# Edge loops of a graph network that load and store two chunks at a time

## The chip, the cores and the metric

The kernel runs on one core of a Trainium2 chip. A core has five engines that each work through a program of their own: TensorE (PE, with its weight loads shown apart as PEld), VectorE (DVE), ScalarE (ACT), GpSimd (POOL) and SyncE (SP, which here only issues DMAs). They wait for each other by semaphores. The metric is the time of one execution in microseconds, lower is better: before the change the median of three runs is 10,185.69 us (10,173.44 to 10,188.64).

## What is computed

A graph has 10,000 nodes and 160,000 edges with 64 features each. The edges come sorted by the node that they point to (`dst`). Two networks run over it, one behind the other. What matters of the reference:

```python
def _genconv(x, src, dst, ea, W1, b1, lg, lb, W2, b2, t):
    m = jax.nn.relu(x[src] + ea) + EPS
    logits = m * t
    mx = jax.ops.segment_max(logits, dst, num_segments=N)
    e = jnp.exp(logits - mx[dst])
    denom = jax.ops.segment_sum(e, dst, num_segments=N)
    alpha = e / denom[dst]
    agg = jax.ops.segment_sum(m * alpha, dst, num_segments=N)
    h = agg + x
    h = h @ W1 + b1
    h = jax.nn.relu(_ln(h, lg, lb))
    return h @ W2 + b2
...
x = x @ encW + encb
ea = edge_attr @ eencW + eencb
x = _genconv(x, src, dst, ea, ...)               # layer 0
for i in range(1, 4):                            # layers 1 to 3
    h = jax.nn.relu(_ln(x, normG[i], normB[i]))
    x = x + _genconv(h, src, dst, ea, ...)
x = jax.nn.relu(_ln(x, normG[0], normB[0])) @ linW + linb
...
# then, with x as it was plus this result, layer-normed and rectified, as h:
score = Kh[src] * Qh[dst] * inv_sqrt_d * Eh      # 8 heads of 8 features
score = jnp.exp(jnp.clip(score.sum(-1, keepdims=True), -5.0, 5.0))
wV = jax.ops.segment_sum(Vh[src] * score, dst, num_segments=n)
```

The output is `x + wV`, 10,000 rows of 64 floats. So there are five passes over all edges: four convolutions with a softmax over the edges of each node, and one attention.

## The kernel before

**Layout.** The edges are cut into two halves. The first half is walked forwards and the second backwards, side by side: a column of a tile holds 64 features of an edge of the first half in partitions 0 to 63, and 64 of an edge of the second in partitions 64 to 127. 128 columns are a group, four groups are a **chunk** (512 columns, 1024 edges). There are 625 groups and so 158 chunks: 155 of four groups, then one of two, one of two and one of one (L51). The function `span` (L759) gives a chunk's first group, its number of groups and its columns.

**Segments.** Maxima and sums over the edges of a node are scans along the columns on DVE. A row of marks, broadcast over 64 partitions for each half, tells the scan where a node ends. After each chunk the scans' states are transposed and written to DRAM as rows (`st0`, or `st1` in attention). When the loop is over, the node stage gathers for each node the row at which its edges ended.

**The stages in order.** A preparation (some 100 us) that finds the ends, then the edge loop of layer 0, a node stage (`node_layer`, L941 on), and so on through layer 3, then the edge loop of attention (`attention_layer`) and a short end.

**A chunk of `softmax_layer`** (L802 on):

- `fetch` (L812): SP loads the marks (`load_marks`, L792: two DMAs, one for each half, six buffers) and either the encoded edges' columns (`load_ea`, L763: one DMA of 256 KB from `eaT`, four buffers) or, in layer 0, the rows of the raw edge attributes (`load_rows`, L769: two DMAs, three buffers `er`).
- in layer 0 alone `turn_rows` (L779): eight matmuls turn the rows into columns in the bank `ept` (L784, L785), ACT copies them to an `ea` buffer (L788), and SP stores that to `eaT` for the layers after it (L789).
- `front` (L821): POOL issues eight indirect DMAs (L756), each of which gathers 128 rows of the nodes' table into one of seven `xg` buffers (a buffer holds a chunk's eight). PE adds the edges times their weights (L829) and the transposed rows (L831) in a PSUM bank `z`. ACT rectifies and scales (L834, L835), DVE scans for the running maximum (L841) with the marks, and ACT makes exponentials (L846 to L849). `z_bank` (L815) takes five banks by turns in layers 1 to 3 (three called `z`, then `ept` and `hist`) and three in layer 0, where the other two have other work.
- `decay` (L856) and `back` (L865), the latter one chunk later: DVE makes the running sums (L871, L874) and transposes them (L900) to one of three buffers `so`, and SP writes these by four DMAs of 128 KB (L904).

**The order.** Within a loop the helper `InOrder` (L79) binds the instructions of each engine to the order in which the program names them, so what is written first is issued first, also on SP. The loop of `softmax_layer` names, for chunk k: the fetch of chunk k+3 (`lead = 3`), the front of k, in layer 0 the turning of k+2, then the back of k-1 with its stores. So on SP the loads for k+3 stand ahead of the stores of k-1. In layer 0 PE and ACT also count nodes and encode them beside the edges; in layer 1 SP writes zeros to `qs` in every fourth chunk (`clear_queries`).

**A chunk of `attention_layer`**: the fetch of chunk k+2 (L1138) is one DMA of the queries' rows (`q`, three buffers under the tag `er`), two of marks and one of `ea`. `ahead` (L1145) turns and spreads the queries of k+1, `fetch_kv` issues eight gathers into four-row halves of the `xg` buffers (`kv`), `scores` (L1180 to L1185) and `weights` (L1191, L1192) make the exponentials, and `back` (L1199 to L1216) makes the running sums and stores them by four DMAs of 64 KB.

**Buffers shared with the node stage.** In `node_layer` the tile `n_g` for the gathered states takes the buffers of `so` (L956).

Of the kernel before, what the change touches and what calls it, by code (L numbers as in the profile page):

```python
# [9 lines left out]
F32 = mybir.dt.float32  # L10
BF = mybir.dt.bfloat16
# [5 lines left out]
P = 128  # L17
# [3 lines left out]
G = 128  # L21
CG = 4
# [4 lines left out]
def kernel(ctx: ExitStack, tc: tile.TileContext, a, out):  # L27
# [24 lines left out]
    NC = len(chunks)  # L52
    W = 1280
# [705 lines left out]
    def span(k):  # L759
        g0, n = chunks[k]  # L760
        return g0, n, slice(g0 * G, (g0 + n) * G)

    def load_ea(k):  # L763
        g0, n, cols = span(k)
        ea = edge.tile([P, CE], F32, name="ea", bufs=4)
        nc.sync.dma_start(ea[:, :n * G], eaT[:, cols])
        return ea

    def load_rows(k, ea_rows):  # L769
        g0, n, cols = span(k)  # L770
        er = edge.tile([P, 2, CG, D], F32, name="er", bufs=3)
        e1 = NE - g0 * G
        nc.sync.dma_start(er[:, 0, :n, :],
                          ea_rows[g0 * G:(g0 + n) * G, :].rearrange("(g p) d -> p g d", p=G))
        nc.sync.dma_start(er[:, 1, :n, :],
                          ea_rows[e1 - n * G:e1, :].rearrange("(g p) d -> p g d", p=G))
        return er

    def turn_rows(k, er):  # L779

        g0, n, cols = span(k)
        pt = ps("ept", [P, CE])
        for g in range(n):
            nc.tensor.matmul(pt[:D, g * G:(g + 1) * G], er[:, 0, g, :], ident, start=True, stop=True)  # L784
            nc.tensor.matmul(pt[D:, g * G:(g + 1) * G], er[:, 1, n - 1 - g, :], anti,  # L785
                             start=True, stop=True)
        ea = edge.tile([P, CE], F32, name="ea", bufs=4)
        nc.scalar.activation(ea[:, :n * G], pt[:, :n * G], AF.Copy)  # L788
        nc.sync.dma_start(eaT[:, cols], ea[:, :n * G])  # L789
        return ea  # L790

    def load_marks(k, rows):  # L792

        g0, n, cols = span(k)
        t = edge.tile([P, CE], BF, name="marks", bufs=6)
        for s in range(2):
            nc.sync.dma_start(t[s * D:(s + 1) * D, :n * G], rows[s:s + 1, cols].to_broadcast([D, n * G]))
        return t
# [3 lines left out]
    def softmax_layer(l, ea_rows=None):  # L802
# [9 lines left out]
        def fetch(k):  # L812
            return load_marks(k, ends_d), load_ea(k) if ea_rows is None else load_rows(k, ea_rows)
# [7 lines left out]
        def front(k, marks, ea):  # L821
            g0, n, cols = span(k)
            m = n * G
            xg = edge.tile([P, CG, 2, D], F32, name="xg", bufs=7)
# [40 lines left out]
        def back(k, z, u, dec, e):  # L865
# [32 lines left out]
            so = edge.tile([P, CE // 32, 2, 32], F32, name="so", bufs=3)  # L898
            for i, t in ((0, se), (1, sm)):
                V.transpose(so[:, :m // 32, i, :], t[:, :m].rearrange("p (b e) -> p b e", e=32))  # L900
            rows_out = st0[2 * g0 * G:2 * (g0 + n) * G, :].rearrange(
                "(b e s) (h x) -> s h e b x", e=32, s=2, h=2)
            for q in range(4):
                nc.sync.dma_start(rows_out[q // 2, q % 2],  # L904
                                  so[q * 32:(q + 1) * 32, :m // 32].rearrange("p b i c -> p b (i c)"))

        order = InOrder()
        def columns_of(k):
            return got[k][1] if ea_rows is None else turn_rows(k, got[k][1])

        lead = 3
        got = [fetch(k) for k in range(lead)]
        eas = [columns_of(k) for k in range(2)]
        held, counts = None, []
        for k in range(NC):
            if k + lead < NC:
                got.append(fetch(k + lead))
            z, u, up, e = front(k, got[k][0], eas[k])
# [21 lines left out]
    def node_layer(l):  # L940
# [13 lines left out]
        @stage  # L954
        def fetch(my, g, i0, n, c):
            my["g"] = t = edge.tile([P, GRP, D2], F32, name="n_g", tag="so", bufs=3)  # L956
            for i in range(n):
                gather(t[:, i, :], st0, ends[:, i0 + i:i0 + i + 1])
            if n % 2:
                V.memset(t[:, n, :], 1.0)  # L960
# [173 lines left out]
    def attention_layer():  # L1134
# [3 lines left out]
        def fetch(k):  # L1138
            g0, n, cols = span(k)
            q = edge.tile([P, CG, 2, D], F32, name="q", tag="er", bufs=3)  # L1140
            nc.sync.dma_start(
                q[:, :n], qs[2 * g0 * G:2 * (g0 + n) * G, :].rearrange("(g p s) d -> p g s d", p=G, s=2))
            return load_marks(k, keeps_d), q, load_ea(k)

        def ahead(k, keep, q, ea):  # L1145

            g0, n, cols = span(k)
            m = n * G
            pq = ps("oe", [P, CE])
# [45 lines left out]
        def back(k, keep, pv, sc):  # L1195
            g0, n, cols = span(k)
            m = n * G
            wv = ps("lg", [P, CE])
# [12 lines left out]
            so = edge.tile([P, CE // 32, 32], F32, name="so1", tag="so", bufs=3)  # L1211
            V.transpose(so[:, :m // 32, :], s[:, :m].rearrange("p (b e) -> p b e", e=32))  # L1212
            rows_out = st1[2 * g0 * G:2 * (g0 + n) * G, :].rearrange(
                "(b e s) (h c) -> s h e b c", e=32, s=2, h=2)
            for q in range(4):
                nc.sync.dma_start(rows_out[q // 2, q % 2], so[q * 32:(q + 1) * 32, :m // 32])  # L1216

        order = InOrder()
        got = [fetch(k) for k in range(2)]
        made = ahead(0, *got[0])  # L1220
        held = None
        for k in range(NC):
            kvs = fetch_kv(k)
            if k + 2 < NC:
                got.append(fetch(k + 2))
# [3 lines left out]
            held = got[k][0], pv, weights(k, psc)  # L1229
            if k + 1 < NC:  # L1230
                made = ahead(k + 1, *got[k + 1])
# [74 lines left out]
```

## Time and profile before

The profiled execution took 10,256.79 us, of which its span, from the first instruction to the last, is 10,254.7 us. The mean granted clock of TensorE in it was 0.629 of full speed.

| | before |
|---|---|
| median of 3 runs | 10,185.69 us |
| profiled execution | 10,256.79 us |
| instructions | 67,417 |
| bytes moved by DMA | 1103.63 MB, mean 108 GB/s |
| packets of the software queue (POOL's gathers) | 215,200, 12.6% of 16 DMA engines' span |
| stores of states, layers 0 to 3 | 2480 DMAs of 128 KB |
| loads of marks, layers 0 to 3 | 1240 DMAs of 64 KB |
| loads of `ea` | 620 DMAs of 256 KB |
| stores of states, attention | 652 DMAs of 64 KB |
| loads of edges' rows (`er`), layer 0 | 310 DMAs of 128 KB |

The counts of DMAs are those that the page lists for chunks of full size; the last three small chunks stand apart in it.

How to read the views. A row of a group names its line, engine and operation, what it writes and reads, how often it ran, its busy time and the mean of one instruction in ns; behind the bar stands the time for which its engine idled just before it, and what ended most of that. "Remote" there means that the releasing event could not be put to an instruction of the trace; "issue" is time in which the engine waited for nothing that the profile shows. A row of a timeline gives the start in us, the time, the engine, the line, the operation, a count, and in brackets the idle time before it. "SPq" is the queue of DMAs that SP issues; the time there is the time for which their issues stretch. A row of windows gives a stretch of time, its length and the busy time of each engine in it, then the granted clock, the busy share of the DMA engines, and GB/s.

### The profile page before, as it was taken

To read this page: it belongs to the slowest core of one execution; us is meant where nothing else is said; L and a number is where in the kernel's file an instruction comes from. 1 tells how busy PE (TensorE), PEld (TensorE's weight loads), DVE (VectorE), ACT (ScalarE), POOL (GpSimd) and SP (SyncE) were. 2 spreads that over 40 slices of the span, in tenths; PEclk is the share of its full clock that TensorE was granted. 3 is DMA by queue.
4 is the path that set the end of the run, shared out by engine and by line. 5 is a ranking of instruction groups with operands and counts; after the bars stand their busy time and mean duration, and the time that the engine had idled before them with its cause. 6 is when DMAs were issued, how large, how long until landed. Compare 5 with 4: busy or idle time off the path is not lost. (4 is left out here: it accounts for less than half of the span.)

```text
span 10254.7 us, 67417 instructions
## 1 busy us (share of the span) xinstructions
PE 4014.2 (39%) x15762; PEld 2685.3 (26%) x15762; DVE 5449.4 (53%) x7473; ACT 2805.0 (27%) x4803; POOL 6358.1 (62%) x6760
## 2 busy tenths in 40 slices
PE   3554445443333333433333343333333444444452
PEld 2333333222222221222222221222222233333331
DVE  3777677535555554355555543555555445545453
ACT  2333333333333333333333342333333310000000
POOL 4566666556666665566666646666666456666665
PEclk6666666665555556665666575555555667777776
DMA  3555555524555554244444433444444235555553
GB/s 89 113 125 123 123 124 123 123 59 119 125 125 129 128 124 109 62 102 105 104 104 103 105 78 71 105 105 104 103 104 106 62 92 122 125 123 126 122 128 82
DMA packets 2462634, 1103.63 MB, mean 108 GB/s; under 512 B 2039472, under 2 KB 2254438, under 8 KB 2462239
## 3 DMA queue, kind: packets, MB, share of 16 engines
q1 hardware_dynamic: 2247039, 827.14, 33.8%
q0 software_dynamic: 215200, 272.11, 12.6%
q8 instruction: 140, 2.29, 0.1%
q14 instruction: 255, 2.09, 0.1%
HBM read 626.51 MB, written 471.91 MB: 107 GB/s over the span
## 5 line engine op out<-in xcount | busy, mean ns | idle before, releaser
L756 POOL DMA_INDIRECT xg<-table,idxA x2500 | 2358.6, 943 | 1916.9 <-remote 829.7
L756 POOL DMA_INDIRECT xg<-table,idxB x2500 | 2358.8, 944 | 763.1 <-issue 761.2
L841 DVE TENSOR_TENSOR_SCAN u<-lg,u,marks 128x512 f32<-128x512 f32 (+1 forms) x628 | 798.5, 1272 | 2721.5 <-ACT lg L835 1612.7
L829 PE MATMUL z<-ea,eencW 128*128 128x512 f32 (+1 forms) x892 | 864.3, 1071 | 2137.1 <-DMA ea<-eaT 898.3
L831 PEld LDWEIGHTS z<-ident,xg 128*128 128x128 f32 x3512 | 800.4, 311 | 591.8 <-issue 566.5
L756 POOL DMA_INDIRECT kv<-kv_table,idxA x625 | 589.5, 943 | 439.7 <-remote 220.2
L831 PE MATMUL z<-ident,xg 128*128 128x128 f32 x3512 | 794.5, 395 | 162.0 <-DMA xg<-table,idxB 85.9
L829 PEld LDWEIGHTS z<-ea,eencW 128*128 128x128 f32 x892 | 222.2, 306 | 2231.8 <-issue 1981.7
L871 DVE TENSOR_TENSOR_SCAN se<-dec,se,e 128x512 f32<-128x512 f32 (+1 forms) x628 | 792.2, 1261 | 0.0
L874 DVE TENSOR_TENSOR_SCAN sm<-dec,sm,me 128x512 f32<-128x512 f32 (+1 forms) x628 | 782.3, 1246 | 0.0
L846 ACT ACTIVATE up<-lg 128x512 f32<-128x512 f32 (+1 forms) x632 | 374.3, 592 | 1352.9 <-issue 693.6
L756 POOL DMA_INDIRECT kv<-kv_table,idxB x625 | 589.7, 944 | 191.1 <-issue 190.2
L834 ACT ACTIVATE lg<-z 128x512 f32<-128x512 f32 (+1 forms) x446 | 249.4, 559 | 1555.8 <-remote 1032.3
L1185 PE MATMUL dec<-eq,head_sum 128*128 128x512 f32 (+2 forms) x316 | 237.1, 841 | 931.2 <-DVE eq L1183 887.1
L1192 ACT ACTIVATE sc<-sc 128x512 f32<-128x512 f32 (+1 forms) x158 | 98.7, 625 | 1744.7 <-DVE sc L1191 685.0
L784 PE MATMUL ept<-ident,er 128*64 128x128 f32 x1250 | 269.3, 380 | 752.4 <-ACT ea L788 517.7
L856 ACT ACTIVATE dec<-up 128x512 f32<-128x512 f32 (+1 forms) x632 | 377.1, 597 | 658.8 <-issue 561.0
L756 POOL DMA_INDIRECT n_g<-st,ends x316 | 300.8, 952 | 403.2 <-issue 142.2
L835 ACT ACTIVATE lg<-lg,teps,tcol 128x512 f32<-128x512 f32 (+1 forms) x632 | 471.4, 746 | 21.1
L829 PE MATMUL hist<-ea,eencW 128*128 128x512 f32 x186 | 189.5, 1123 | 709.5 <-DMA ea<-eaT 286.6
L829 PE MATMUL ept<-ea,eencW 128*128 128x512 f32 x186 | 185.5, 1100 | 710.3 <-DMA ea<-eaT 286.4
L1156 DVE TENSOR_TENSOR_SCAN qh<-marks,qh,oe 128x512 f32<-128x512 bf16 (+1 forms) x157 | 198.6, 1265 | 488.6 <-remote 389.8
(285 smaller groups left out, 8704.9 us busy)
## 6 DMA issues: line engine op xcount, KB each, us to landing
st<-so SPq DMA_DIRECT2D x2480, 128.0 KB
ea<-eaT SPq DMA_DIRECT2D x620, 256.0 KB
marks<-ends_d SPq DMA_DIRECT2D x1240, 64.0 KB
st<-so SPq DMA_DIRECT2D x652, 64.0 KB
xg<-table,idxA POOLq DMA_INDIRECT x2500
xg<-table,idxB POOLq DMA_INDIRECT x2500
qs<-zeros SPq DMA_DIRECT2D x40, 1000.0 KB
er<-in_edge_attr_dram SPq DMA_DIRECT2D x310, 128.0 KB
```

Of the source, the lines that this page charges most:

```text
L756: nc.gpsimd.indirect_dma_start(out=t, out_offset=None, in_=table, in_offset=bass.IndirectOffsetOnAxis(ap=idx, axis=0))
L784: nc.tensor.matmul(pt[:D, g * G:(g + 1) * G], er[:, 0, g, :], ident, start=True, stop=True)
L829: nc.tensor.matmul(z[:, :m], eencW, ea[:, :m], start=True, stop=False)
L831: nc.tensor.matmul(z[:, g * G:(g + 1) * G], xg[:, g, :, :].rearrange("p s d -> p (s d)"), ident, start=False, stop=(g == n - 1))
L834: S.activation(lg[:, :m], z[:, :m], AF.Relu)
L835: S.activation(lg[:, :m], lg[:, :m], AF.Identity, bias=teps[:, l:l + 1], scale=tcol[:, l:l + 1])
L841: V.tensor_tensor_scan(u[:, 1:m + 1], lg[:, :m], marks[:, :m], last, op0=OP.max, op1=OP.add)
L846: S.activation(up[:, :m], lg[:, :m], AF.Relu)
L856: S.activation(dec[:, :m], up[:, :m], AF.Exp, scale=-1.0)
L871: V.tensor_tensor_scan(se[:, :m], dec[:, :m], e[:, :m], prev.get("e", zero1), op0=OP.mult, op1=OP.add)
L874: V.tensor_tensor_scan(sm[:, :m], dec[:, :m], me[:, :m], prev.get("m", zero1), op0=OP.mult, op1=OP.add)
L1185: nc.tensor.matmul(psc[:, :m], head_sum, eq[:, :m], start=True, stop=True)
```

## The change

The chunks are put together in **units**: 78 pairs, and the last two chunks each alone, 80 in all. Loads and stores go by units, the computation still by chunks. `reach` gives a unit's first group, its groups and its columns; `within` gives the columns that a chunk has in a tile of its unit; `is_first` and `is_last` tell where in its unit a chunk stands.

- The tiles `ea`, `er`, `marks`, `q` and `so` are twice as long. Their buffers: `ea` 3 (before 4), `er` and `q` 2 (before 3), `marks` 3 (before 6), `so` 2 (before 3).
- In the loops, two units are fetched ahead of the first chunk; the fetch of unit u+2 is named at the last chunk of unit u, ahead of that chunk's front.
- `turn_rows` writes one half of a pair's `ea` at each chunk, and stores the pair's columns at its last chunk.
- The states of a pair are stored at its last chunk, by four DMAs of twice the size.
- `n_g` takes the buffers of `ea` in place of those of `so`.

The PE, ACT, DVE and POOL instructions of a chunk are the same as before, on slices of the longer tiles.

```diff
+    units = [[k, k + 1] for k in range(0, NC - 2, 2)] + [[NC - 2], [NC - 1]]
+    unit_of = {k: u for u, ks in enumerate(units) for k in ks}
...
-    def load_ea(k):
-        g0, n, cols = span(k)
-        ea = edge.tile([P, CE], F32, name="ea", bufs=4)
+    def reach(u):
+
+        g0 = chunks[units[u][0]][0]
+        n = sum(chunks[k][1] for k in units[u])
+        return g0, n, slice(g0 * G, (g0 + n) * G)
+
+    def within(k):
+
+        c = (chunks[k][0] - chunks[units[unit_of[k]][0]][0]) * G
+        return slice(c, c + chunks[k][1] * G)
+
+    def is_first(k):
+        return units[unit_of[k]][0] == k
+
+    def is_last(k):
+        return units[unit_of[k]][-1] == k
+
+    def load_ea(u):
+        g0, n, cols = reach(u)
+        ea = edge.tile([P, 2 * CE], F32, name="ea", bufs=3)
         nc.sync.dma_start(ea[:, :n * G], eaT[:, cols])
         return ea
 
-    def load_rows(k, ea_rows):
-        g0, n, cols = span(k)
-        er = edge.tile([P, 2, CG, D], F32, name="er", bufs=3)
+    def load_rows(u, ea_rows):
+        g0, n, cols = reach(u)
+        er = edge.tile([P, 2, 2 * CG, D], F32, name="er", bufs=2)
...
-    def turn_rows(k, er):
+    def turn_rows(k, er, ea):
 
         g0, n, cols = span(k)
+        in_unit = within(k)
+        first, total, unit_cols = reach(unit_of[k])
+        at = g0 - first
         pt = ps("ept", [P, CE])
         for g in range(n):
-            nc.tensor.matmul(pt[:D, g * G:(g + 1) * G], er[:, 0, g, :], ident, start=True, stop=True)
-            nc.tensor.matmul(pt[D:, g * G:(g + 1) * G], er[:, 1, n - 1 - g, :], anti,
+            nc.tensor.matmul(pt[:D, g * G:(g + 1) * G], er[:, 0, at + g, :], ident, start=True, stop=True)
+            nc.tensor.matmul(pt[D:, g * G:(g + 1) * G], er[:, 1, total - 1 - at - g, :], anti,
                              start=True, stop=True)
-        ea = edge.tile([P, CE], F32, name="ea", bufs=4)
-        nc.scalar.activation(ea[:, :n * G], pt[:, :n * G], AF.Copy)
-        nc.sync.dma_start(eaT[:, cols], ea[:, :n * G])
+        if ea is None:
+            ea = edge.tile([P, 2 * CE], F32, name="ea", bufs=3)
+        nc.scalar.activation(ea[:, in_unit], pt[:, :n * G], AF.Copy)
+        if is_last(k):
+            nc.sync.dma_start(eaT[:, unit_cols], ea[:, :total * G])
         return ea
 
-    def load_marks(k, rows):
-
-        g0, n, cols = span(k)
-        t = edge.tile([P, CE], BF, name="marks", bufs=6)
+    def load_marks(u, rows):
+
+        g0, n, cols = reach(u)
+        t = edge.tile([P, 2 * CE], BF, name="marks", bufs=3)
...
         def front(k, marks, ea):
             g0, n, cols = span(k)
             m = n * G
+            ea, marks = ea[:, within(k)], marks[:, within(k)]
...
-            so = edge.tile([P, CE // 32, 2, 32], F32, name="so", bufs=3)
+            if is_first(k):
+                prev["so"] = edge.tile([P, 2 * CE // 32, 2, 32], F32, name="so", bufs=2)
+            so, to = prev["so"], within(k)
             for i, t in ((0, se), (1, sm)):
-                V.transpose(so[:, :m // 32, i, :], t[:, :m].rearrange("p (b e) -> p b e", e=32))
-            rows_out = st0[2 * g0 * G:2 * (g0 + n) * G, :].rearrange(
+                V.transpose(so[:, to.start // 32:to.stop // 32, i, :],
+                            t[:, :m].rearrange("p (b e) -> p b e", e=32))
+            if not is_last(k):
+                return
+            first, total, _ = reach(unit_of[k])
+            rows_out = st0[2 * first * G:2 * (first + total) * G, :].rearrange(
                 "(b e s) (h x) -> s h e b x", e=32, s=2, h=2)
...
-        lead = 3
-        got = [fetch(k) for k in range(lead)]
-        eas = [columns_of(k) for k in range(2)]
+        got, eas = [fetch(u) for u in range(2)], []
+        for k in range(2):
+            eas.append(columns_of(k))
         held, counts = None, []
         for k in range(NC):
-            if k + lead < NC:
-                got.append(fetch(k + lead))
-            z, u, up, e = front(k, got[k][0], eas[k])
+            if is_last(k) and unit_of[k] + 2 < len(units):
+                got.append(fetch(unit_of[k] + 2))
+            z, u, up, e = front(k, got[unit_of[k]][0], eas[k])
...
-            my["g"] = t = edge.tile([P, GRP, D2], F32, name="n_g", tag="so", bufs=3)
+            my["g"] = t = edge.tile([P, GRP, D2], F32, name="n_g", tag="ea", bufs=3)
...
-            q = edge.tile([P, CG, 2, D], F32, name="q", tag="er", bufs=3)
+            q = edge.tile([P, 2 * CG, 2, D], F32, name="q", tag="er", bufs=2)
...
-            so = edge.tile([P, CE // 32, 32], F32, name="so1", tag="so", bufs=3)
...
+            if is_first(k):
+                prev["so"] = edge.tile([P, 2 * CE // 32, 32], F32, name="so1", tag="so", bufs=2)
...
         for k in range(NC):
             kvs = fetch_kv(k)
-            if k + 2 < NC:
-                got.append(fetch(k + 2))
+            if is_last(k) and unit_of[k] + 2 < len(units):
+                got.append(fetch(unit_of[k] + 2))
```

## The prediction

> **What bounds the kernel now.** I read the page first, then stretches by window, then the timelines of SP and POOL, then the waits. The page alone:
>
> ```profile
> span 10254.7 us, 67417 instructions
> PE 4014.2 (39%) x15762; PEld 2685.3 (26%) x15762; DVE 5449.4 (53%) x7473; ACT 2805.0 (27%) x4803; POOL 6358.1 (62%) x6760
> q1 hardware_dynamic: 2247039, 827.14, 33.8%
> L756 POOL DMA_INDIRECT xg<-table,idxA x2500 | 2358.6, 943 | 1916.9 <-remote 829.7
> L829 PE MATMUL z<-ea,eencW 128*128 128x512 f32 (+1 forms) x892 | 864.3, 1071 | 2137.1 <-DMA ea<-eaT 898.3
> ```
>
> POOL is the busiest engine, and nearly all it does is to issue row gathers at 943 ns. PE's largest idle time ends when a load of `ea` lands, and SP issues those. One window for each edge loop (layers 0 to 3, then attention) shows how near POOL is to being the limit:
>
> ```profile
> core 0: us, PE busy (x) PEld busy (x) DVE busy (x) ACT busy (x) POOL busy (x), PEclk, DMA share, GB/s
> 99.50:1956.20 1856.70, 885.59 (x5240) 633.47 (x5240) 1244.53 (x1819) 620.12 (x1062) 1178.44 (x1249) 0.64 0.54 118
> 2172.00:3953.40 1781.40, 564.79 (x1518) 365.15 (x1518) 921.23 (x1196) 539.71 (x902) 1178.32 (x1249) 0.56 0.50 121
> 4171.00:5946.50 1775.50, 566.99 (x1518) 367.63 (x1518) 921.35 (x1196) 539.54 (x902) 1178.49 (x1250) 0.60 0.44 100
> 6168.30:7944.50 1776.20, 568.30 (x1520) 367.93 (x1521) 922.19 (x1196) 539.55 (x902) 1179.27 (x1250) 0.56 0.44 100
> 8300.50:10112.00 1811.50, 878.62 (x4310) 650.56 (x4310) 904.24 (x1069) 96.34 (x153) 1180.17 (x1251) 0.73 0.52 124
> ```
>
> The five loops fill 9001 of 10,255 us. Each has 1250 gathers. Back to back they start 1.247 us apart (943 ns and 0.30 us between two), so 1250 take 1559 us: that is a loop's floor, 9.98 us for a chunk of eight. Length less floor is what can be won: 297 (of which about 74 lie before the first chunks flow), 222, 216, 217 and 252 us, 1204 in all. No other engine is near: DVE has 921 of 1776 us. What are POOL's pauses? Layer 2 in time, POOL and then SP:
>
> ```profile
> 4728.33 0.94 POOL L756 DMA_INDIRECT xg<-table,idxA  x1 [0.30 <-issue]
> 4729.58 0.94 POOL L756 DMA_INDIRECT xg<-table,idxB  x1 [0.30 <-issue]
> 4739.15 0.94 POOL L756 DMA_INDIRECT xg<-table,idxA  x1 [8.62 <-remote]
> ...
> 4719.71 5.65 SPq L904 DMA_DIRECT2D st<-so  x4
> 4725.38 1.46 SPq L797 DMA_DIRECT2D marks<-ends_d  x2
> 4728.92 0.71 SPq L766 DMA_DIRECT2D ea<-eaT  x1
> 4732.43 4.25 SPq L904 DMA_DIRECT2D st<-so  x4
> 4737.43 0.71 SPq L797 DMA_DIRECT2D marks<-ends_d  x2
> 4738.84 0.01 SPq L766 DMA_DIRECT2D ea<-eaT  x1
> 4746.51 2.25 SPq L904 DMA_DIRECT2D st<-so  x4
> 4748.81 1.29 SPq L797 DMA_DIRECT2D marks<-ends_d  x2
> 4750.20 0.52 SPq L766 DMA_DIRECT2D ea<-eaT  x1
> ```
>
> POOL runs six chunks and stops 8.6 us, because all seven `xg` buffers wait for PE. SP needs 12.7 us from one chunk's stores to the next (4719.7 to 4732.4) while POOL runs, and 7 us for the same seven DMAs (4746.5 to 4753.4) just after POOL has paused. So in layers 1 to 3 SP, at 12.7 us a chunk, is slower than POOL at 9.98, and PE gets `ea` at SP's pace. In layer 0 and attention SP has gaps and is not late: there SP's waits are for ACT's `ea` (570 us) and DVE's `so` (502 us).
>
> **The change, part by part.**
>
> *SP's DMAs, halved in number.* A chunk of layers 1 to 3 now costs SP 4 stores, 2 marks, 1 `ea`; layer 0 adds 2 `er` and 1 `eaT` store, attention adds 1 `q`: 7, 9 and 8 DMAs. With 80 units for 158 chunks they become 560 instead of 1106 in a loop of layers 1 to 3, 720 instead of 1422, 640 instead of 1264: 2964 fewer. An issue does not cost by its packets: the medians are 692 ns for a store (512 packets), 698 ns for marks (64), 586 ns for `ea` (128). So SP's slow pace falls from 12.7 us a chunk to about 6.4, below POOL's 9.98, and `ea` stops being late. What is late next is POOL itself and what makes it pause.
>
> Here a rule speaks against the change. The Trainium skill, "DMA: Bandwidth & Descriptors", section "Issuing engines are not separate DMA queues", holds that the sequencer's time to start a DMA is usually small beside the DMA. By that rule the 2964 issues hide and the sum is 0. The SP rows above say 12.7 us a chunk where POOL needs 9.98, so in layers 1 to 3 I follow the row; in layer 0 and attention, where SP idles, the rule stands for the issue time itself.
>
> *POOL's pauses.* Does removing SP's lateness remove the pauses? Not by itself. In the last fence PE had issued its matmuls on `ept` at 4704.4 (PE timeline), yet ACT's relu on that bank started at 4738.9, after 15.6 us of idling for "remote", 7 us after POOL stopped: results of PE become visible late while POOL runs without a break. Two bounds. If the pauses go with SP's DMA count (1.5 us in layer 0 for 9 DMAs, 1.37 for 7 in layers 1 to 3, 1.55 for 8 in attention: 0.17 to 0.20 us each), half of 1150 us goes: -575. If they are POOL's own, 0. The nearest rows are stretches with other DMA rates; the share of time POOL pauses beyond its 1.247 us steps, from POOL counts in windows and SP's timeline:
>
> - start of layer 2, 4172 to 4329.6 us: 112 gathers, 42 SP DMAs, 0.27 a us: 0.113
> - rest of layer 2: 1135 gathers, 990 DMAs, 0.61 a us: 0.122
> - attention from 8353 us: 1214 gathers, 0.69 a us: 0.139
> - layer 0 from 173 us: 1193 gathers, 0.75 a us: 0.165
>
> After the change all loops issue 0.31 to 0.38 DMAs a us, between the first two rows. I take 0.113 for layers 1 to 3 and the middle, 0.1175, for the others: 3 x 1778 x 0.0095 = 51; layer 0 1783 x 0.0475 = 85; attention 1759 x 0.0215 = 38. Sum **174 us**, far nearer the lower bound than -575, since the start of layer 2 pauses nearly as much with few DMAs.
>
> *Data.* Same bytes; rows of `ea` double to 4 KB and marks to 2 KB, the store rows stay 256 bytes. q1 has 24.7 ns a packet (33.8% of 16 engines' 10,255 us over 2.247 M). 90,000 packets fewer free 0.9% of the engines, which are 44 to 54% busy: 0 on the path. A doubled store of 1024 packets holds the engines 1.6 us instead of 0.8.
>
> *Stores moved to the second chunk of a pair.* Nobody reads `st` before the loop ends. The last two units are single chunks, so the tail is as before: 0.
>
> *Lead.* Before, chunk k+3 was fetched in iteration k, behind the stores of k-2. Now unit u+2 is fetched at the pair's second chunk, behind the stores of u-1: its first chunk is as far ahead as before, the second one chunk further. But four doubled stores stand ahead in the queue: 4 x 0.8 = 3.2 us later, in layer 0 also two `er` of 0.8 more: 4.8 us (estimates from q1). In layers 1 to 3 five z banks give PE's next `ea` five chunks' time: 0. In layer 0 (three banks, `er` two pairs deep) PE waited for `er` 39 times, 106.8 us; I count 0 there in the forecast because the second chunk of each pair no longer waits (gain at most 53 us against at most 39 x 4.8 = 187 lost); this cover is the rival below.
>
> *Buffers.* `so` two pairs (four chunks, before three), marks three pairs (six, as before), `q` and `er` two pairs (four, before three), `ea` three pairs: none tighter, and the reader of the oldest is done before SP reaches the fetch. `n_g` moves from `so` to `ea`: its first gathers wait for all stores either way; the next loop's first two `ea` loads wait for the last `n_g` to be divided, which ends some 20 us before the loop. 0. DVE, ACT and PE run the same instructions.
>
> The sum is against the profiled execution (10,256.8 us with its ends); the median of the runs is 0.7% lower, so 174 becomes 173 and 10,185.7 becomes **10,013**; I say 10,010.
>
> **Rivals.**
>
> *SP was the limit all along.* For it: in loop 2 PE waits for `ea` or marks before almost every chunk, SP is the only engine with a pace over 11.4 us. Against it: layer 0 and attention pause more, with SP idle. Then the pauses halve: 10,186 - 571 = 9615.
>
> *Slower: the first chunk of each pair in layer 0 comes late.* The queue is in order, so `er` of the pair stands behind four doubled stores and feeds PE's turn, which stands ahead of the next z. At the 39 waits of today, 4.8 us each: +187, so 10,375; if all 79 pairs wait 7.5 us, +486. It decides once the delay exceeds what seven gathered `xg` chunks cover for POOL. Against it: layer 0 paces at 11.6 us and three banks leave over 20 us from one fetch to its use.
>
> *Nothing.* The pauses are POOL's and the DMA counts do not matter: 10,186.
>
> **How the numbers follow.** Forecast 0.36, SP the limit 0.23, slower 0.30, nothing 0.11. No change means within 0.2%, about what three runs that agree within 15 us can tell. Of "nothing", 0.06 stays within, 0.03 falls faster and 0.02 slower: faster 0.62, same 0.06, slower 0.32. The range reaches past 9615 on one side and to 10,380 on the other, leaving out the far ends of the two outer cases, some 0.2 together.
>
> **What would show it.** SP's rows per pair: four stores, two marks, one `ea` within 13 us, in 22 us. PE's wait for `ea` in layers 1 to 3 mostly gone. If POOL's 8.6 us pauses stay, still 12% of a loop, with PE's relu waits on "remote", the pauses are POOL's own; if they halve, SP's count was the cause. Wrong would be a layer 0 window above 1857 us with PE waiting for `er` more than 250 us, or loops 1 to 3 under 1690 us.

## The result: no gain

The changed kernel takes 10,193.33 us in the median of 12 runs (10,180.23 to 10,211.44), beside 10,185.64 us of 12 runs before. The ratio is 1.0009 with a 95% interval of 1.0000 to 1.0018: about 8 us longer if anything, where 173 us less were forecast. In the sittings of this study the kernel before took from 10,180 to 10,254 us, so a ratio is always to the runs of its own sitting. The profile of before that stands above took 10,256.79 us, longer than all 12 of these runs; a second one (run before_again below) took 10,177.53 us and is the one to set beside the profile after, 10,180.23 us.

From the page of the changed kernel, the rows that answer to those shown of before:

```profile
span 10178.3 us, 61984 instructions
PE 3875.6 (38%) x15762; PEld 2575.4 (25%) x15762; DVE 5448.0 (54%) x7473; ACT 2803.8 (28%) x4803; POOL 6360.2 (62%) x6760
q1 hardware_dynamic: 2099775, 826.95, 34.3%
L759 POOL DMA_INDIRECT xg<-table,idxA x2500 | 2358.5, 943 | 1853.3 <-issue 671.8
```

The change does what it says: 5433 instructions fewer, 3803 of them SP's (2964 DMAs, as counted, the rest semaphore instructions), and 147,264 packets fewer on SP's queue at the same bytes. POOL's gathers still take 943 ns each, and POOL idles nearly as long ahead of them. One window for each edge loop of the changed kernel, from first to last gather (length, then busy time of each engine, clock, DMA share, GB/s):

```profile
99.70:1930.20 1830.50, 866.81 (x5240) 616.79 (x5240) 1242.67 (x1820) 618.91 (x1063) 1179.54 (x1250) 0.65 0.57 120
2164.50:3926.60 1762.10, 526.11 (x1518) 334.40 (x1518) 924.48 (x1199) 540.78 (x905) 1179.23 (x1250) 0.58 0.50 122
4148.90:5914.60 1765.70, 518.94 (x1518) 331.50 (x1518) 919.14 (x1192) 537.83 (x899) 1179.25 (x1250) 0.59 0.43 100
6135.00:7901.80 1766.80, 523.19 (x1538) 334.13 (x1538) 922.28 (x1196) 539.66 (x902) 1179.27 (x1250) 0.59 0.44 100
8252.00:10039.90 1787.90, 889.84 (x4311) 656.56 (x4312) 908.25 (x1073) 96.34 (x153) 1180.40 (x1251) 0.73 0.52 126
```

From first to last gather, in us, beside the second profile of before:

| loop | before_again | after | from its last gather to the next stage's first, before_again | after |
|---|---|---|---|---|
| layer 0 | 1827.7 | 1829.5 | 56.5 | 67.0 |
| layer 1 | 1768.3 | 1761.1 | 54.3 | 55.4 |
| layer 2 | 1764.0 | 1764.6 | 54.2 | 58.9 |
| layer 3 | 1763.1 | 1765.8 | 54.3 | 54.8 |
| attention | 1790.4 | 1786.9 | 29.7 | 28.1 |

The loops did not move (8913.5 against 8907.9 us in sum), though SP has half as many DMAs in each. What moved most is the stretch behind layer 0, by 10.5 us. So there are two questions: why do POOL's pauses not care for SP, and what became late behind layer 0?

Here is how a pause of the changed kernel looks, in layer 2: rows from the timelines of SP, of PE and of POOL.

```profile
4461.26 3.47 SPq L936 DMA_DIRECT2D st<-so  x4
4464.77 2.63 SPq L822 DMA_DIRECT2D marks<-ends_d  x2
4467.52 0.84 SPq L786 DMA_DIRECT2D ea<-eaT  x1
4504.00 3.41 SPq L936 DMA_DIRECT2D st<-so  x4
```

```profile
4480.16 2.08 PE L855 MATMUL z<-ea,eencW 128*128 128x512 f32 x2 [4.69 <-issue]
4482.03 0.42 PE L857 MATMUL z<-ident,xg 128*128 128x128 f32 x1
4483.79 0.37 PE L857 MATMUL z<-ident,xg 128*128 128x128 f32 x1 [1.34 <-issue]
4485.89 0.37 PE L857 MATMUL z<-ident,xg 128*128 128x128 f32 x1 [1.73 <-issue]
...
4495.68 0.37 PE L857 MATMUL z<-ident,xg 128*128 128x128 f32 x1 [0.82 <-issue]
```

```profile
4487.98 0.94 POOL L759 DMA_INDIRECT xg<-table,idxB  x1 [0.30 <-issue]
4496.64 0.94 POOL L759 DMA_INDIRECT xg<-table,idxA  x1 [7.71 <-PE z L857]
```

SP issues nothing between 4468 and 4504, so its issues hold nobody up there. `ea` was there: PE's first matmul of the chunk runs at 4480. Yet its eight matmuls on `xg`, which take 1.05 us elsewhere in the same loop, take 14 us, with idle time that ends in "issue", that is, nothing that the profile shows.

And what does POOL wait for? It stops ahead of the loop's chunk 31 (the first is 0), which takes the `xg` buffer that chunk 24 had, seven before it. PE's matmuls on chunk 24, and ACT's first instruction on it:

```profile
4460.74 1.91 PE L857 MATMUL hist<-ident,xg 128*128 128x128 f32 x8
4496.40 0.58 ACT L860 ACTIVATE lg<-hist 128x512 f32<-128x512 f32 x1 [13.29 <-PE z L857]
```

PE had read the buffer by 4462.7, before POOL stopped at all. ACT idles for 13 us and begins on that chunk at 4496.4 and POOL goes on at 4496.6, both 34 us after PE's end. So POOL does not wait for PE to read; what PE has done is seen late. It is so at all 27 pauses over 1 us that stand ahead of a chunk of this layer: POOL goes on 31 to 74 us after PE's last read of the buffer. ACT starts 26 us after PE's last matmul on its chunk in the median of this layer, and 74 at most. The rows themselves are not late: by the packets of the software queue a gather is complete 2.2 us after its start in the median of this layer, and 4.2 at most.

### The profile page after: what moved, and what is told of

Its sections match the earlier page's. It is cut to its first block, busy times and chain, and to the rows that moved or that the text cites. A ratio compares the mean times of both kernels' runs of the same rounds, so it can differ in the third digit from the quotient of the medians.

```text
span 10178.3 us, 61984 instructions
## 1 busy us (share of the span) xinstructions
PE 3875.6 (38%) x15762; PEld 2575.4 (25%) x15762; DVE 5448.0 (54%) x7473; ACT 2803.8 (28%) x4803; POOL 6360.2 (62%) x6760
## 4 chain that ended last, share of the span: by engine, by line
issue 27%; DVE 21%; another core or an unknown queue 14%; POOL 11%; PE 10%; SPq 9%; ACT 4%; DMA 3%; DVEq 0%; ACTq 0%; POOLq 0%
POOL xg L759 10%; SPq L936 4%; DVE u L867 3%; SPq L822 3%; DVE sm L900 3%; DVE so L928 2%; DVE lg L869 2%; DVE se L897 2%; PE dec L1222 2%; PE z L1217 2%; DVE me L895 1%; PE oe L1188 1%; DVE qh L1193 1%; PE z L857 1%
## 5 line engine op out<-in xcount | busy, mean ns | idle before, releaser
L855 PE MATMUL z<-ea,eencW 128*128 128x512 f32 (+1 forms) x892 | 811.9, 1010 | 1866.4 <-issue 954.9
L857 PEld LDWEIGHTS z<-ident,xg 128*128 128x128 f32 x3512 | 753.4, 286 | 869.2 <-issue 827.1
L869 DVE TENSOR_TENSOR lg<-lg,u 128x512 f32<-128x512 f32 (+1 forms) x632 | 438.2, 693 | 21.9
L471 DVE TENSOR_TENSOR onehot_lo<-oe,lo_b 128x640 bf16<-128x640 f32 (+1 forms) x278 | 205.7, 740 | 429.2 <-remote 406.6
```

What stands on the lines that cost most here:

```text
L855: nc.tensor.matmul(z[:, :m], eencW, ea[:, :m], start=True, stop=False)
L857: nc.tensor.matmul(z[:, g * G:(g + 1) * G], xg[:, g, :, :].rearrange("p s d -> p (s d)"), ident, start=False, stop=(g == n - 1))
L869: V.tensor_sub(lg[:, :m], lg[:, :m], u[:, 0:m])
```

## The experiments

Two theories follow. **SP**: the packets of SP's DMAs (the stores are still 2048 packets a chunk) hold PE up. **POOL**: its own stream of gathers does, whatever SP issues. Most kernels below use layers 1 to 3 as three arms, since these loops are alike (1761, 1765 and 1766 us). Lengths are from a loop's first gather to its last.

**before_again**: the kernel before, unedited.

> The kernel before, profiled once more, to see how far two profiles of the same kernel differ. Every theory: the five edge loops (first to last gather) again near 1857, 1780, 1774, 1774 and 1810 us; if the whole is near the median of 10,186 us instead of 10,257, each loop may be some 14 us shorter (70 us over five loops).

10,177.53 us; the table above has its loops. They are 10 to 29 us shorter than in the first profile, more than the expected 14 in layer 0 and attention, less in layers 1 to 3.

**sp_off**: layer 1 stores nothing, layer 2 loads marks and `ea` once, layer 3 does neither.

```diff
+        kept = []
+
         def fetch(u):
+            if l in (2, 3):
+                if not kept:
+                    kept.append((load_marks(u, ends_d), load_ea(u)))
+                return kept[0]
...
-            if not is_last(k):
+            if not is_last(k) or l in (1, 3):
                 return
```

> The changed kernel with three arms, one in each of the layers 1 to 3 (it leaves out work there, so what these layers compute is not the reference's): layer 1 stores no states; layer 2 loads marks and ea once and uses them for all units; layer 3 does neither, so that SP has next to nothing to do. Changed kernel: 1761, 1765 and 1766 us from first to last gather. Theory SP (packets of SP's DMAs hold up PE and so POOL; the change halved DMAs but left 2048 store packets a chunk): layer 3 falls to the floor of POOL, 1560 to 1610 us, layer 1 most of the way, layer 2 stays. Theory POOL (POOL's own stream of gathers slows what PE's results take to be seen, whatever SP does): all three stay within 30 us of 1765.

Windows of its layers 1 to 3:

```profile
2164.80:3924.20 1759.40, 621.90 (x1539) 387.80 (x1540) 924.67 (x1199) 541.89 (x905) 1179.61 (x1250) 0.54 0.30 79
4097.60:5849.70 1752.10, 622.44 (x1548) 388.75 (x1548) 927.36 (x1203) 543.57 (x908) 1179.53 (x1250) 0.54 0.32 68
6081.90:7838.40 1756.50, 625.17 (x1538) 389.40 (x1538) 922.94 (x1196) 540.77 (x902) 1179.44 (x1250) 0.54 0.12 24
```

In layer 3 the DMA engines are busy for 12% of the time in place of 44%, with almost nothing but gathers, and the loop is 10 us shorter. POOL's pauses are still there (195 us). The theory SP falls for layers 1 to 3. For layer 0 and attention no run takes SP's DMAs away; there the change itself, which halves them, is the test, and it moved their loops by less than 4 us.

**pool_arms**: layer 1 gathers for every second chunk only, layer 2 gets a small memset on POOL ahead of each gather, in layer 3 PE turns one of four groups.

```diff
+            if l == 1 and not is_first(k):
+                xg = prev["xg"]
+            else:
...
+                        if l == 2:
+                            nc.gpsimd.memset(filler, 0.0)
...
-            for g in range(n):
+            for g in range(n if l != 3 else 1):
...
```

> The changed kernel with three arms (it leaves out work in layers 1 and 3): layer 1 gathers only for the first chunk of each pair, the second uses the same rows; layer 2 gathers all, with a small memset on POOL ahead of each of the 1250 gathers; layer 3 gathers all, but PE turns only one of four groups. Changed kernel: 1761, 1765 and 1766 us. Theory POOL (a backlog that fills while POOL issues gathers without a break, drained at about one gather in 1.41 us): layer 1 falls under 1250 us; in layer 2 the memsets take the place of the pauses, the loop stays within 60 us of 1765 and pauses over 1 us fall under 60 us in sum; layer 3 falls under 1650 only if PE's number of instructions is what fills the backlog, else it stays within 30 us. Theory SP: layer 2 becomes longer by all its memsets (at an estimated 0.2 us each +250, so 2015) and layer 3 stays.

1063.3, 1771.0 and 1723.2 us. Layer 1 speaks for POOL. Layer 2 says less than was meant: the memset of 127 ns fits into the 0.30 us between two gathers, POOL's step became 1.255 us, and pauses over 1 us still make 112. Layer 3 fell into neither number: 43 us shorter, no pause over 1 us, and POOL's median step was 1.397 us. Relieved of PE, POOL did not run at 1.247: it became slow itself.

**knee**: one, two and three memsets of 128x160 ahead of each gather.

```diff
+                    for _ in range(l):
+                        nc.gpsimd.memset(filler, 0.0)
                     gather(xg[:, g, s, :], tables[l], index(g0 + g, s))
```

> The changed kernel with POOL slowed by memsets of 128x160 ahead of each gather: one in layer 1, two in layer 2, three in layer 3 (their time is not known; by the 128x16 memset at 127 ns some 0.28 us each is an estimate, which makes POOL's step between gathers about 1.40, 1.75 and 2.1 us where it was 1.247). Theory POOL (a gather costs about 1.405 us in the long run, 1761 to 1766 us for 1250, and a burst at 1.247 is only borrowed): a loop takes the larger of 1760 us and 1250 of its own steps: layer 1 about 1760 without pauses over 1 us (under 60 us in sum), layers 2 and 3 their steps, 2190 and 2620, without pauses, and PE's and SP's slow steps gone there. Rival (the pauses come from PE's own lateness, a fixed share of about 12% of the time): each loop takes its own steps plus 12%: 1970, 2450, 2940.

Windows of its layers 1 to 3 (POOL's count has the memsets in it):

```profile
2164.80:3936.60 1771.80, 510.12 (x1519) 322.18 (x1520) 927.34 (x1203) 547.18 (x908) 1498.02 (x2500) 0.59 0.47 122
4148.30:6265.00 2116.70, 741.55 (x1560) 379.08 (x1560) 957.32 (x1243) 567.92 (x937) 1787.78 (x3749) 0.50 0.35 86
6448.80:8932.40 2483.60, 743.98 (x1562) 379.04 (x1562) 957.84 (x1244) 568.80 (x938) 2077.20 (x4997) 0.50 0.30 73
```

The steps came out at 1.362, 1.644 and 1.934 us. Layer 1 has 319 us more work on POOL than the changed kernel and is 10 us longer: its pauses fell from 201 to 43 us. Layers 2 and 3 take 1250 of their steps (2055 and 2418) and 61 and 65 us, without the 12% that the rival asked for. So there is a knee: below a step of about 1.4 us POOL's own pace does not matter, above it the loop goes by POOL's step. And the late signals are gone there. PE's end of a chunk and ACT's start on it in layer 3:

```profile
6814.46 0.77 PE L859 MATMUL z<-ident,xg 128*128 128x128 f32 x2 [3.21 <-DMA xg<-table,idxB]
6815.27 0.58 ACT L862 ACTIVATE lg<-z 128x512 f32<-128x512 f32 x1 [7.34 <-PE z L859]
```

ACT starts 0.04 us after PE's end. That is also the median in layers 2 and 3; in layer 1 it is 22 us, and in the changed kernel's layer 2 it was 26.

**gather_arms**: six, ten and eight gathers a chunk; in layer 3 PE reads none of them.

```diff
...
+            kept = 3 if l == 1 else n
-            for g in range(n):
+            for g in range(min(n, kept)):
...
+            if l == 2:
+                more = edge.tile([P, 2, D], F32, name="more", bufs=7)
+                for s in range(2):
+                    gather(more[:, s, :], tables[l], index(g0, s))
...
-            for g in range(n):
+            for g in range(n if l != 3 else 0):
...
```

> The changed kernel with three arms (it leaves out work in layers 1 and 3): layer 1 gathers six of a chunk's eight (the fourth group takes the third's rows), layer 2 gathers ten (two go to a tile that nobody reads), layer 3 gathers eight that PE does not read (no matmul on xg at all). Theory POOL, 1.405 us for a gather: layer 1 about 938 x 1.405 = 1320, layer 2 about 1566 x 1.405 = 2200, layer 3 about 1250 x 1.405 = 1755 although nothing waits for its gathers. Rival PE (POOL pauses because PE frees xg late): layer 3 falls to POOL's own 1250 x 1.247 = 1560, and layer 2 is between 1953 (1566 x 1.247) and 1990, since the two more gathers give PE the time that it lacks.

1335.3 us for 940 gathers, 2205.0 for 1566, 1730.2 for 1250 that nobody waits for: 1.421, 1.408 and 1.384 us each, as the theory POOL said and far from the rival's 1560 in layer 3. The work of the other engines in each chunk is not what makes the price: of the changed kernel's layer 2 some 203 us lie over 1250 steps of 1.249, and if these went by chunks, 940 gathers would take an estimated 1378 us and 1566 take 2160, not 1335 and 2205. Layer 3 shows the price by itself. Four windows of 100 us from its start; POOL's count is the gathers begun:

```profile
6142.30:6242.30 100.00, 19.46 (x25) 6.14 (x23) 70.92 (x91) 42.62 (x73) 75.66 (x80) 0.60 0.51 117
6242.30:6342.30 100.00, 18.45 (x20) 5.87 (x20) 57.23 (x72) 31.70 (x55) 75.69 (x80) 0.53 0.44 101
6442.30:6542.30 100.00, 18.46 (x20) 5.86 (x20) 57.06 (x72) 32.00 (x54) 76.18 (x72) 0.55 0.43 101
7700.00:7800.00 100.00, 18.75 (x20) 5.86 (x20) 55.26 (x72) 30.83 (x53) 76.57 (x72) 0.53 0.45 105
```

For 200 us POOL begins 80 gathers in 100 us (1.251 us each), then 72 to the end of the loop (the mean of the rest is 1.407 us). It looks as if a backlog ended the burst: 160 gathers at 1.251 where 1.407 can be kept up leave about 18 owed. It is not one of rows: in this layer too a gather is complete 2.3 us after its start in the median and 4.3 at most. What is owed, no run shows. With PE reading, the time is lost in pauses instead.

**row_arms**: 64 rows for each gather, rows of 128 bytes, and the same rows again and again.

```diff
...
+                    if l == 1:
+                        gather(xg[:D, g, s, :], tables[l], index(g0 + g, s)[:D])
+                    elif half:
+                        gather(xg[:, g, s, :],
+                               tables[l].rearrange("n (a d) -> (n a) d", a=2), index(g0 + g, s))
+                    else:
+                        gather(xg[:, g, s, :], tables[l], index(g0 + g if l == 0 else 0, s))
...
```

> The changed kernel with three arms, all with eight gathers a chunk (their data is not the reference's): layer 1 gathers 64 rows instead of 128 with each, layer 2 gathers 128 rows of 128 bytes instead of 256, layer 3 gathers the rows of the first group again and again. Changed kernel: 1761, 1765 and 1766 us. If a gather's price goes with its rows, layer 1 falls under 1300 or to the pace of the other engines (about 1063 where half of the gathers were left out). If it goes with bytes, layers 1 and 2 both fall. If with which rows are read, layer 3 falls alone. If it goes with the instruction alone, all three stay within 40 us of 1765.

Windows of its layers 1 to 3:

```profile
2160.70:3927.60 1766.90, 647.79 (x1518) 356.99 (x1518) 921.18 (x1195) 538.95 (x902) 1124.37 (x1250) 0.50 0.45 109
4146.80:5909.10 1762.30, 511.06 (x1518) 329.20 (x1518) 919.18 (x1192) 538.49 (x899) 1179.29 (x1250) 0.58 0.40 88
6128.80:7896.40 1767.60, 512.50 (x1518) 328.69 (x1518) 919.17 (x1192) 538.03 (x899) 1179.35 (x1250) 0.60 0.43 100
```

1.41 us for a gather in all three, though layer 1's gathers were issued 1.204 us apart. Within these sizes the price is the instruction's: not rows, not bytes, not where the rows lie.

**fetch_early**: the convolutions fetch unit u+2 at the first chunk of unit u.

```diff
-            if is_last(k) and unit_of[k] + 2 < len(units):
+            if is_first(k) and unit_of[k] + 2 < len(units):
```

> The changed kernel with one edit: in the convolution layers unit u+2 is fetched at the first chunk of unit u instead of the last, one chunk earlier. Theory POOL plus a late er (in the changed kernel the drain of layer 0 after its last gather is some 10 us longer, since PE waits up to 12.8 us for a pair's er): the time from layer 0's last gather to layer 1's first falls from 235 to about 225 us, the loops stay at 1829, 1761, 1765, 1766 and 1787 within 15 us, and the whole is some 10 us shorter than the changed kernel, about 10,183, ratio to before 0.999 to 1.000. Rival (lead matters in the loops as well): layer 0's loop itself falls by over 30 us.

10,162.35 us (9 runs; before 10,185.79), ratio 0.998 (0.997 to 0.999): a little faster than before, and more than the 0.999 to 1.000 that was expected. PE's waits for `ea` and `er` in the changed kernel and then in this one (total us, times, longest):

```profile
PE z L855 <- DMA ea<-eaT: 733.4, 57, 22.7
PE hist L855 <- DMA ea<-eaT: 281.3, 20, 22.8
PE ept L855 <- DMA ea<-eaT: 236.0, 16, 24.8
PE ept L807 <- DMA er<-in_edge_attr_dram: 128.2, 18, 12.8
```

```profile
PE z L855 <- DMA ea<-eaT: 129.9, 25, 9.9
PE hist L855 <- DMA ea<-eaT: 39.9, 8, 6.6
PE ept L807 <- DMA er<-in_edge_attr_dram: 17.7, 1, 17.7
PE ept L855 <- DMA ea<-eaT: 14.2, 3, 5.4
```

Over 1000 us of waiting for `ea` and 110 for `er` are gone, and the loops stand at 1835.7, 1761.1, 1761.2, 1756.5 and 1792.5: the wait that was PE's largest cost nothing. What came back is the drain of layer 0. The first gather of its node stage, in before_again, the changed kernel and this one (idle time before it in brackets):

```profile
1982.99 0.94 POOL L756 DMA_INDIRECT n_g<-st,ends  x1 [55.58 <-DVE u L840]
```

```profile
1996.22 0.94 POOL L759 DMA_INDIRECT n_g<-st,ends  x1 [66.04 <-DVE u L866]
```

```profile
1991.64 0.94 POOL L759 DMA_INDIRECT n_g<-st,ends  x1 [55.37 <-DVE u L866]
```

In the stretch behind layer 0 that is the 10 us expected. By the ratios the gain over the changed kernel is 0.3%, some 29 us, and the two profiles differ by 13; where the rest lies is open.

**paced**: one memset of 128x190 to 128x220 ahead of every gather, attention's too.

```diff
+                    nc.gpsimd.memset(filler[:, :(220, 190, 205, 220)[l]], 0.0)
                     gather(xg[:, g, s, :], tables[l], index(g0 + g, s))
```

> The changed kernel with a memset of POOL ahead of each gather that brings POOL's own step to about the 1.407 us that gathers take in the long run: width 220 in layer 0 and attention (step about 1.415), 190, 205 and 220 in layers 1 to 3 (1.39, 1.40, 1.415). Theory POOL: pauses over 1 us vanish in layers 1 to 3, a loop keeps its 1760 to 1780 us, but PE no longer lags seven chunks behind, so that the stretch from a loop's last gather to the next stage's first falls by 30 us or so for each of the five loops, as it did after the slowed layers 2 and 3 (221 to 185, 351 to 318 us): about 10,193 - 150 = 10,040, faster than both kernels. Rival PE (pauses come from PE's lateness and add to POOL's steps): loops near 1.41 x 1250 x 1.12 = 1970, the whole about 11,200.

10,180.97 us, ratio 0.9994 (0.9986 to 1.0003), so no gain that can be told from none, where 10,040 us were expected. The loops are as said (1771.0, 1767.5 and 1770.5, pauses over 1 us down to 21, 10 and 5): POOL's idling was filled with work at no cost. But the stretch after the last gather fell by 11 to 17 us in layers 1 to 3 where 30 were expected. At a step so near 1.407 us the lateness is not worked off: ACT still starts 23.5, 23.9 and 7.4 us after PE's end in the median of these layers.

**taper**: fetch_early, and two memsets of 128x160 ahead of each gather in the last 8, 14 and 20 chunks of layers 1 to 3.

```diff
+                    if k >= NC - (0, 8, 14, 20)[l]:
+                        nc.gpsimd.memset(filler, 0.0)
+                        nc.gpsimd.memset(filler, 0.0)
```

> fetch_early, and two memsets of 128x160 ahead of each gather in the last 8 chunks of layer 1, the last 14 of layer 2 and the last 20 of layer 3 (POOL's step there 1.64 us instead of 1.41 in the mean). Theory POOL with a backlog at the loop's end (PE seven chunks behind, 54 us from the last gather to the node stage's first): the loops become longer by 0.23 us for each slowed gather at most, 15, 26 and 37 us, and less where the backlog had to be paid anyway; the stretch after the last gather falls from 54 towards the 16 us that the wholly slowed layers showed. Best for layer 1 or 2: a gain of 10 to 20 us each, the whole at about 10,162 - 30 = 10,130. Rival (the end is set by DVE's and ACT's work on the last chunks, whatever POOL did before): no gain, 10,162 plus the slowed steps, some 10,230.

10,201.00 us beside 10,254.05 in this sitting: 0.9945 (0.9931 to 0.9958). From last gather to node stage 17.6, 16.9 and 16.5 us in place of 55.3, 54.4 and 51.8. The number of slowed chunks does not matter for that, but the loops grow with it, to 1786.3, 1797.6 and 1809.8 us, so fewer should do.

**taper_short**, with **after_again** (the changed kernel, unedited) in the same sitting: the last 8, 5, 8 and 6 chunks of layers 0 to 3.

```diff
-                    if k >= NC - (0, 8, 14, 20)[l]:
+                    if k >= NC - (8, 5, 8, 6)[l]:
```

> As taper, with the last 8 chunks slowed in layer 0, 5 in layer 1, 8 in layer 2 and 6 in layer 3. Theory POOL with a backlog at the end: in taper the loops grew with the number of slowed chunks and the stretch after the last gather was 17 us whether 8, 14 or 20 were slowed; so fewer slowed chunks cost less, and the stretch stays under 25 us down to the point at which PE no longer catches up. Expected: layers 2 and 3 some 30 us shorter each than in fetch_early (loop and stretch together), layer 1 with 5 chunks between 15 and 30, layer 0 some 20; the whole at a ratio to before of about 0.989 to 0.992. Rival (no gain from fewer): the ratio stays at taper's 0.9945 or goes back to fetch_early's 0.998.

> The changed kernel, profiled on the same chip as taper_short: its stretches from a loop's last gather to the node stage's first, to be compared on one chip: 66, 55, 55, 55 and 29 us within 4 us, loops within 1% of 1829, 1761, 1765, 1766 and 1787.

10,137.77 us beside 10,238.08: **0.9908 (0.9892 to 0.9925)**, faster than both kernels by 0.9%. after_again took 10,229.61 in one run, with loops of 1843.2, 1770.7, 1770.5, 1768.9 and 1800.6. Layer 2's drain in after_again and in taper_short:

```profile
5994.12 0.94 POOL L759 DMA_INDIRECT n_g<-st,ends  x1 [55.98 <-DMA marks<-ends_d]
```

```profile
5912.64 0.94 POOL L759 DMA_INDIRECT n_g<-st,ends  x1 [16.82 <-issue]
```

The loop is 9 us longer (1779.5 against 1770.5), the stretch behind it 39 shorter. With 5 chunks (layer 1) it is 34.8, with 6 (layer 3) 24.9: about 8 are needed to catch up, a little more than the seven that POOL is ahead of ACT at most. Loop and drain together gained 30 us in layer 2, 31 in layer 0, 28 in layer 3 and 18 in layer 1: 107 us in sum, where the spans of the two profiles differ by 109 (10,227.7 against 10,118.3). fetch_early is part of this edit, and some 10 us of layer 0's 31 are its.

## Why the prediction was wrong, step by step

- **The floor.** "Back to back they start 1.247 us apart, so 1250 take 1559 us: that is a loop's floor." This is the term that carried everything, and it was mis-sized: 1.247 is the spacing in a burst. In the long run a gather takes 1.407 us (layer 3 of gather_arms), which makes 1759 us, and layers 1 to 3 took 1761 to 1766. Of the 1204 us "that can be won", 5 x 200 = 1000 were never there.
- **POOL's pauses.** The step that failed: the pauses were priced by the share of time that POOL pauses at different rates of SP's DMAs, and 174 us taken from that. The four rows differed in their loops' other work and in how long POOL had run when they began, not through SP. With SP at 0.31 DMAs a us (after) or nearly none (sp_off) a gather still takes 1.41 us, and the five loops together moved by 6 us of 8900 when SP's DMAs were halved. The bound at 0 was the right end.
- **"... because all seven `xg` buffers wait for PE."** They did not. PE was done with the buffer that POOL took next at 4708.1, 31 us before POOL went on at 4739.15:

```profile
4706.22 1.92 PE L831 MATMUL ept<-ident,xg 128*128 128x128 f32 x8
4738.91 0.58 ACT L834 ACTIVATE lg<-ept 128x512 f32<-128x512 f32 x1 [15.64 <-remote]
```

- **"Results of PE become visible late while POOL runs without a break."** This was seen and written down, but as a mark of POOL's pauses, not as the cause to be measured. It was the clue: POOL and ACT go on together, 8.4 us (not 7) after POOL's last gather ended.
- **SP's DMAs halved.** The count was right. SP's pace was misread: the 12.7 us from one chunk's stores to the next are a distance, in a loop that takes 11.2 us a chunk in the mean, and the issues in them make 7.8 us (5.65, 1.46 and 0.71); for the rest SP idled. So SP was not slower than POOL. After the change a pair's seven DMAs take 7.1 us (4461.26 to 4468.36), 3.6 us a chunk where 6.4 was said. That `ea` "stops being late" did not come: PE still waited 1251 us for it (1471 and 1663 in the two profiles of before). fetch_early removed most of that and gained nothing by it in the loops. An engine's wait is no cost where the engine behind which all stand is bound by something else. The rule of the Trainium skill that was set against this step ("DMA: Bandwidth & Descriptors", section "Issuing engines are not separate DMA queues") gave a sum of 0 and was right about the sum. The row that was followed instead is one of an engine off the path.
- **Data.** The 90,000 packets fewer were 147,264: 99,840 of data, and 16 packets of 4 bytes for each of the 2964 DMAs, which were left out. On the path it made no difference.
- **Stores, lead, buffers: 0 each.** Right in the loops. "The tail is as before: 0" was wrong behind layer 0, by 10.5 us: in the drain POOL no longer covers, DVE's chunks follow each other at 6.9 us, and PE waits up to 12.8 us for the pair's `er`, which is issued behind four doubled stores. fetch_early, which issues it a chunk earlier, took the 10 us back. This is the rival's mechanism, at the one place where its cover is gone; over the whole of layer 0, where POOL binds, it cost nothing (PE's waits for `er` are 128 us in before_again and after).
- **The rival "nothing"**, held at 0.11, was the case that came, for the reason that it gave: the pauses are POOL's. Why a gather costs 1.407 us stays open. "SP was the limit all along" falls with sp_off.

## What to carry to other kernels

The distance between two instructions in a burst is not a rate, and the distance between two turns of a loop is not a cost: take an engine's pace over a stretch long enough to have a pause in it, leave its idle time out of its work, and let the candidate run with nobody waiting for it, as in layer 3 of gather_arms, before calling its pauses waste. A wait that is large in the list is worth its time only if the loop is not paced by another engine; one run of the loop with that transfer left out tells it. Where an engine waits for another, compare when the other was done: 34 us between the two said more than the releaser's name. And where one engine paces a long loop and the others lag behind it, the end of the loop is the place for a gain: slowing POOL for the last eight chunks gave 30 us in layer 2, which no edit to the loop's middle did.

## What was not expected of the hardware

A row gather on POOL has two prices: 943 ns and a gap, 1.20 to 1.25 us from one to the next, for a burst of some 160 at most, and 1.407 us after that, about the same for 64 or 128 rows and for 128 or 256 bytes. POOL has room for 0.26 us of other work for each gather at a cost of 10 us in 1761 (knee, layer 1).

Beyond that burst ACT and POOL learn late of what PE has done: ACT by 26 us in the median of the changed kernel's layer 2, and by 0.04 us where POOL's step is 1.64 us (knee). PE goes slowly too, as its rows at 4482 to 4496 show: from the second matmul on, starts are multiples of 0.70 us apart (2.10 for the next two rows). The records of semaphore updates in the trace show the same beat: in layers 1 to 3 of the changed kernel the median is 7.5 to 8 in 5 us (7 is one per 0.70 us), and 64 and 61 in the layers of knee in which POOL's step was 1.64 and 1.93. These records are not whole: for the same chunks they number about 4000 a layer in the changed kernel and over 31,000 in these two layers of knee, so idle time that ends in "issue" may have had a releaser that was not recorded. Whether the recording of the profile itself has a part in the beat, no run tells.

Twice 0.70 is 1.40, the price of a gather. That a gather is paid for by two such beats fits these numbers but was not shown: no run here changed what a gather does to semaphores or queues other than by its number, its rows and its bytes, and none changed the number of `xg` buffers.
